# Two more products of the second feed-forward matmul split a second time, in five of eight blocks

## The chip, the core and the metric

The kernel runs on one core of a Trainium2 chip. Its engines are called PE (TensorE, matmuls), DVE (VectorE), ACT (ScalarE), POOL (GpSimd) and SP (SyncE, which here only issues DMAs). All five take their own instructions in order and wait for each other through semaphores. The metric is device time in microseconds (us). "Span" is the time from the first to the last instruction of the profiled execution.

## What is computed

One conditioned transformer block over x of shape (2, 2048, 512) in float32, with weights that the inputs give:

```python
emb = jnp.dot(jax.nn.silu(t), ada_w) + ada_b
shift_msa, scale_msa, gate_msa, shift_mlp, scale_mlp, gate_mlp = jnp.split(emb, 6, axis=-1)
norm = _ln(x) * (1.0 + scale_msa[:, None]) + shift_msa[:, None]
h = jax.nn.gelu(jnp.dot(norm, ssm_w1) + ssm_b1, approximate=False)
ssm_out = jnp.dot(h, ssm_w2) + ssm_b2
x = x + gate_msa[:, None] * ssm_out
norm2 = _ln(x) * (1.0 + scale_mlp[:, None]) + shift_mlp[:, None]
hf = jax.nn.gelu(jnp.dot(norm2, ff_w1) + ff_b1, approximate=True)
ff_out = jnp.dot(hf, ff_w2) + ff_b2
x = x + gate_mlp[:, None] * ff_out
```

ssm_w1 and ssm_w2 are 512 x 512, ff_w1 is 512 x 1024, ff_w2 is 1024 x 512.

## The kernel before

The 4096 rows are cut into 8 blocks of 512; blocks 0 to 3 belong to the first batch row, 4 to 7 to the second. The gates of a batch row are multiplied into ssm_w2 and ff_w2, so that the weights are reloaded and folded once in between. The order of the work is written out by hand (`manual_schedule`): what is emitted first stands first in its engine's queue.

All matmuls are float32, and none is done in the plain way. A product of two matrices, each cut into quarters, is made from seven products P1 to P7 of sums of quarters instead of eight. Sums of operands are made by POOL or DVE (`sums_of_first`, `sums_of_second`, 4 instructions each); the seven results are added up in PSUM banks y, x and v, which are read while they grow: `ORDER` gives the order P1, P2, P6, P5, P7, P3, P4 and `BANK` the bank of each. Some banks are "seeded": ACT writes the bias row into them first (`seed`).

Four stages make a block, and in the loop over i (blocks 1 to 7) those of different blocks are interleaved, in this order on PE:

- hC of block i, the first feed-forward layer (`Second.products`), by 26 products out of a deeper scheme. Their operands, 20 "forms", are made by `sums_of_registers` from the normalised block. DVE and ACT add the results up (lines 895 and 898), and ACT applies the gelu (876).
- oA of block i+1, the second matmul of the SSM part with its residual (`residual`).
- oC of block i, the second feed-forward matmul with its residual (`residual_in_leaves`, or `residual` in block 0).
- hA of block i+2, the first matmul of the SSM part (`First`).

So the residual stage oC of block 6 is followed by hC of block 7 at once, since there is no block 8.

In oC, `residual_in_leaves` makes P1, P5 and P6 as plain products (8 matmuls of 128 x 256 results each, line 724), each read by DVE (735). P2, P3 and P4 are split once more in the same manner. Each then has seven "leaves" of two matmuls with 128 x 128 results (757). They go in seven rounds of the order `LEAVES`: round 0 has the leaf P1 of all split products, round 1 the leaf P2, and so on. After P2's and P3's leaf DVE reads both (773), after P4's leaf it reads that (776). P7 is plain; its 8 matmuls are spread over rounds 0 to 3, and DVE reads it in round 4. The operand sums of the leaves are made by `leaves_of_weight` (once per batch row, into `fw2_t`) and `leaf_sums` (per block, into room in `forms`, or two `big` tiles in block 6).

"Hooks" are lists of instructions that are emitted behind a named product or round: `hook(hooks, ("P7",), ops)`. By them the other blocks' work is placed: statistics of the two normalisations (499, 500), their scales on POOL (508 to 526), the normalisation on ACT (539), transposes on DVE (550), the moves (559, 16 DMAs, SBUF to SBUF, that finish the transpose), the modulation on ACT (582), operand sums (347), forms (819), loads and stores on SP (203, 805).

x of a block is loaded once (203) and kept in a tile of the pool `big` (8 slots) until the block's result is stored; the normalised form nT gets a slot of its own. Other tiles of `big` are hA, hClo, hChi and, at the start, the ada weights.

## Time and profile before

| what | us |
|---|---|
| median of 3 runs | 594.32 |
| lowest and highest | 593.11, 594.48 |
| the profiled execution | 592.64 |
| its span | 590.8 |
| PE busy in it | 581.2 |
| DVE, ACT, POOL busy | 402.6, 236.0, 396.1 |

In block 2 the four stages last, and keep the engines busy, as follows (stretches of the span; POOL's spans are rough):

| stage | from, to | length | DVE | ACT | POOL |
|---|---|---|---|---|---|
| oA of block 3 | 223.50, 235.58 | 12.08 | 5.62 | 4.44 | 10.66 |
| oC of block 2 | 235.58, 258.77 | 23.19 | 15.32 | 6.70 | 9.58 |
| hA of block 4 | 258.77, 270.87 | 12.10 | 9.06 | 4.33 | 9.33 |
| hC of block 3 | 270.87, 293.35 | 22.48 | 15.34 | 15.29 | 22.01 |

PE is busy through the whole of each. In the rows of the profile a line's columns are the source line, the engine, the operation, the tile written and the tiles read, shapes, the count, busy time and mean duration; in a timeline the first two numbers are the start and the length, and the bracket is the idle time before it and what ended it. PE's matmuls overlap in the records, so that their price is the distance between starts.

### The profile page before, as it was taken

Reading aid. Unit: us, or ns where it says so; the run is one execution under the profiler, and the core shown is the slowest. Engines: PE = TensorE matmul, PEld = TensorE weight load, DVE = VectorE, ACT = ScalarE, POOL = GpSimd, SP = SyncE. Lnnn points to the kernel's source line nnn. Section 1 sums busy time; section 2 is a strip of 40 time slices with the busy share of each in tenths; the row PEclk is TensorE's granted clock in tenths of the full one; section 3 lists DMA queues with packets and bytes.
Section 4 is the critical chain, followed back from the end, with each engine's and each line's share of the span. In section 5 each row is a group of like instructions: output and inputs, shape, how many; then the busy total and the mean of one; then the engine's idle time right before and its main releaser. Section 6 shows DMA issues by size and latency. Waiting matters only on the chain.

```text
span 590.8 us, 8982 instructions
## 1 busy us (share of the span) xinstructions
PE 581.2 (98%) x3127; PEld 512.9 (87%) x3127; DVE 402.6 (68%) x723; ACT 236.0 (40%) x400; POOL 396.1 (67%) x480
## 2 busy tenths in 40 slices
PE   7999999999999999999999999999999999998997
PEld 4888888888889888998889988898888988897886
DVE  4978888897567475675755778874756446569663
ACT  2235457305532364234721456124553236222420
POOL 1875359999980968539984599948687294804260
PEclk9999999999999999999999999999999999999999
DMA  8990333300324104440152702231030400031002
GB/s 317 395 388 11 86 72 79 101 37 36 72 73 116 46 0 103 155 136 2 24 137 60 226 1 50 94 72 72 1 72 1 143 2 1 1 72 71 1 1 72
DMA packets 24376, 50.17 MB, mean 85 GB/s; under 512 B 4576, under 2 KB 5644, under 8 KB 23436
## 3 DMA queue, kind: packets, MB, share of 16 engines
q1 hardware_dynamic: 20608, 44.86, 24.5%
q10 hardware_dynamic: 3724, 4.75, 3.3%
q8 instruction: 25, 0.41, 0.3%
q14 instruction: 19, 0.16, 0.1%
HBM read 26.51 MB, written 8.40 MB: 59 GB/s over the span
## 4 chain that ended last, share of the span: by engine, by line
PE 95%; DVE 2%; DMA 2%; SPq 0%; issue 0%
PE py_oC L724 12%; PE px_hC L881 10%; PE py_hA L465 9%; PE py_oA L465 9%; PE py_hC L881 8%; PE pv_hC L881 8%; PE pl_oC_P_y L757 6%; PE pv_hA L465 5%; PE pv_oA L465 5%; PE pv_oC L724 4%; PE pl_oC_P_v L757 3%; PE px_hA L465 2%; PE py_oC L465 2%; PE py_hC L465 2%; PE px_oA L465 2%; DMA ada<-in_L_cond_ada_w_dram 2%
## 5 line engine op out<-in xcount | busy, mean ns | idle before, releaser
L582 ACT ACTIVATE nT<-nT,mod,mod 128x512 f32<-128x512 f32 x54 | 39.6, 803 | 103.0 <-DMA nT<-blocks 54.1
L539 ACT ACTIVATE nT<-x,nmr,rstd 128x512 f32<-128x512 f32 x56 | 42.5, 804 | 52.9 <-POOL nmr L526 38.0
L724 PE MATMUL py_oC<-fw,hClo 128*128 128x256 f32 x224 | 54.1, 379 | 0.0
L508 POOL TENSOR_SCALAR ve<-mv 128x4 f32<-128x4 f32 x16 | 3.7, 232 | 72.4 <-DVE mv L500 65.7
L499 DVE BATCH_NORM_STATS2 st<-x 128x6 f32<-128x512 f32 x64 | 43.4, 678 | 5.2 <-DMA x<-in_x_dram 4.9
L347 POOL TENSOR_TENSOR hSC<-hClo,hChi 128x512 f32<-128x512 f32 (+1 forms) x17 | 20.5, 1213 | 37.9 <-ACT hChi L876 24.4
L724 PEld LDWEIGHTS py_oC<-fw,hClo 128*128 128x128 f32 x224 | 40.4, 190 | 4.3
L881 PE MATMUL py_hC<-forms,fw 128*128 128x256 f32 x168 | 40.8, 379 | 0.0
L898 DVE TENSOR_TENSOR hClo<-hClo,py_hC 128x512 f32<-128x512 f32 x42 | 28.5, 681 | 17.3 <-ACT hClo L895 9.6
L819 POOL TENSOR_TENSOR forms<-forms 128x256 f32<-128x256 f32 x51 | 38.1, 748 | 3.0
L550 DVE STREAM_TRANSPOSE blocks<-nT 128x512 f32<-128x512 f32 x56 | 38.0, 695 | 1.6 <-ACT nT L539 1.2
L819 POOL TENSOR_TENSOR forms<-nT,forms 128x256 f32<-128x256 f32 x38 | 27.7, 749 | 15.9 <-DVE forms L819 15.4
L881 PEld LDWEIGHTS py_hC<-forms,fw 128*128 128x128 f32 x168 | 31.8, 190 | 4.4
L687 DVE TENSOR_TENSOR x<-py_oA,x 128x512 f32<-128x512 f32 x32 | 22.0, 688 | 19.4 <-PE py_oA L465 14.3
L898 DVE TENSOR_TENSOR hChi<-hChi,pv_hC 128x512 f32<-128x512 f32 x35 | 23.3, 683 | 14.3 <-PE pv_hC L881 14.3
L465 PE MATMUL py_hA<-nT,w 128*128 128x256 f32 x128 | 30.4, 380 | 0.0
L881 PE MATMUL px_hC<-forms,fw 128*128 128x256 f32 x112 | 27.8, 380 | 2.1 <-DVE forms L819 2.1
L876 ACT ACTIVATE hClo<-hClo,colsT 128x256 f32<-128x256 f32 x56 | 25.3, 500 | 4.9 <-DVE hClo L898 4.4
L895 ACT ACTIVATE hClo<-px_hC 128x512 f32<-128x512 f32 x21 | 12.5, 597 | 35.0 <-PE px_hC L881 30.1
L465 PE MATMUL py_oA<-w,hA 128*128 128x256 f32 x112 | 26.5, 379 | 0.0
L465 PEld LDWEIGHTS py_hA<-nT,w 128*128 128x128 f32 x128 | 23.7, 190 | 3.1 <-DVE hA L639 0.2
L876 ACT ACTIVATE hChi<-hChi,colsT 128x256 f32<-128x256 f32 x56 | 25.1, 496 | 1.9 <-DVE hChi L898 1.9
(291 smaller groups left out, 1584.0 us busy)
## 6 DMA issues: line engine op xcount, KB each, us to landing
nT<-blocks SPq DMA_DIRECT2D x168, 64.0 KB
x<-in_x_dram SPq DMA_DIRECT2D x7, 1024.0 KB
out_dram<-x SPq DMA_DIRECT2D x14, 512.0 KB
ada<-in_L_cond_ada_w_dram SPq DMA_DIRECT2D x6, 1024.0 KB
fw<-in_L_cond_ff_w_dram SPq DMA_DIRECT2D x2, 2048.0 KB
nT<-blocks ACTq DMA_DIRECT2D x56, 64.0 KB
w<-in_L_cond_ssm_w_dram SPq DMA_DIRECT2D x3, 1024.0 KB
fw<-in_L_cond_ff_w_dram SPq DMA_DIRECT2D x2, 1024.0 KB
```

The lines of the kernel that those rows point to most:

```text
L465: nc.tensor.matmul(ps[b][j * apart][:, j, :], lhs(p, j, k), rhs(p, j, k), start=(fresh and j * (not apart) == 0 and k == 0), stop=(p in (" ...
L499: nc.vector.bn_stats(st, xs[self.i][:, c, :])
L539: nc.scalar.activation(t, x_c, AF.Identity, bias=self.nmr[:, c : c + 1], scale=self.rstd[:, c : c + 1])
L550: nc.vector.transpose(self.bl[:, :, :, c, :].rearrange("p m k q -> p k m q"), self.nT[:, c, :].rearrange("p (k m q) -> p k m q", k=KD, m=C),)
L582: nc.scalar.activation(dst, src, AF.Identity, bias=shift, scale=scale)
L687: nc.vector.tensor_tensor(d, ps[BANK[p]][:, js], d, ALU.add)
L724: yield lambda j=j, k=k: nc.tensor.matmul(ps[BANK[p]][:, j, :], hops(p, j, k), wops[p][:, k, :], start=False, stop=(k == kdim - 1), skip_g ...
L757: nc.tensor.matmul(t[:, n, :], hops.leaves["P4" if which == "P4" else ("P2", "P3")[n]][f][:, k, :], leaf_wops["P4" if which == "P4" else ( ...
L819: eng.tensor_tensor(reg[d], reg[a], reg[b], ALU.add if f == "+" else ALU.subtract)
L876: nc.scalar.activation(h, h, AF.Gelu_apprx_tanh, bias=fb1T[:, m : m + 1])
L881: nc.tensor.matmul(ps[b][:, j, :], fa[ra][:, j * P : (j + 1) * P], fb[rb].rearrange("p a (c q) -> p c a q", q=Q), start=(fresh and j == 0) ...
L898: nc.vector.tensor_tensor(dest(d), dest(d), ps[b], op)
```

## The change

- In blocks 2, 3, 5, 6 and 7 (`five`) P5 and P7 are split into leaves too. Only P1 and P6 stay plain; P6 stands behind round 0. A round has ten matmuls; all leaves of a round are emitted first, then the readings. P5's leaves are read into two places with one instruction, as are P7's; P1+P6 goes into the lower rows with one wide instruction behind round 2. Blocks 1 and 4 keep three split products.
- P7's leaves share P4's banks. P5's chain has a part of the seeded bank v and parts of P4's banks; ACT writes a bias row (`leaf_row`, made by `apart_leaves`) into P4's bank v.
- Operand sums: P5's are made together with P3's, behind the scales of the second normalisation; P7's (`sums7`) are made by POOL in oA, in blocks 6 and 7 by DVE. The weight's new sums (`later`) are made by DVE in the following hA and hC.
- From block 2 on, the first normalisation writes into the tile of x itself. x is loaded again at the start of hC (`load_x(i + 1)`). The first load moves from P1 to P5 of oC. `big` has 7 slots; `brows` lies in `fw2_t`.
- Moved: the statistics of the first normalisation from oC to hA, its scales to hC, its normalisation and transposes to later places in hC; the modulation of the second one and its transposes to other places in oC; the reload of ff_w2 behind the last leaves; all 20 forms of block 7 into oC of block 6, 4 on DVE and 16 on POOL (12 and 8 before). In hA ACT takes the first reads of P6 and P5.

The diff, cut to its core:

```diff
-    big = ctx.enter_context(tc.tile_pool(name="big", bufs=8))
+    big = ctx.enter_context(tc.tile_pool(name="big", bufs=7))
...
+        for j, (p, w) in enumerate((("P4", s[:, 2]), ("P5", s[:, 0]), ("P7", lo[:, :, D // 2 :]))):
+            q, t = {n: v[:, :, 0, :] for n, v in views(w).items()}, thirds(fw2_t[:, 2 + j])
+            ops[p] = second_operands(q, t)
+            sums[p] = sums_of_second(q, t, engs[p])
...
+    def apart_leaves(row, eng):
+        a, b = slice(D // 2, D // 2 + P), slice(D // 2 + P, D)
+        eng.tensor_tensor(leaf_row[:, 2], row[:, b], row[:, a], ALU.subtract)
...
-                self.nT = big_tile(f"nT{self.name}")
+                in_place = self.which == 1 and self.i >= 2
+                self.nT = xs[self.i] if in_place else big_tile(f"nT{self.name}")
...
+        place = {("P2", b): (rooms["P23", b], 0) for b in "yxv"}
+        place |= {("P3", b): (rooms["P23", b], 1) for b in "yxv"}
+        place |= {("P4", b): (rooms["P4", b], 0) for b in "yxv"}
+        place |= {("P7", b): (rooms["P4", b], 1) for b in "yxv"}
+        place |= {("P5", "y"): (seeded, 0), ("P5", "v"): (rooms["P4", "v"], 2), ("P5", "x"): (rooms["P4", "x"], 2)}
...
+        if five:
+            places = {1: ("P6",), 2: ("P5",), 3: ("R2",), 4: ("P7",), 5: ("R4", "P3"), 6: ("P4",)}
         for r, f in enumerate(LEAVES):
             t, e = LEAF_AT[f]
-            for n in range(2):
-                leaf("P23", n, f)
-            d = xt[:, t, :].rearrange("p (q d) -> p q d", q=2)[:, :, e * P : (e + 1) * P]
-            nc.vector.tensor_tensor(d, leaf_ps["P23", LEAF_BANK[f]][:, :2, :], d, ALU.add)
-            leaf("P4", 0, f)
-            d = xt[:, 2 + t, e * P : (e + 1) * P]
-            nc.vector.tensor_tensor(d, leaf_ps["P4", LEAF_BANK[f]][:, 0, :], d, ALU.add)
-            if r == read_p7:
+            for p in ("P2", "P3"):
+                leaf(p, f)
+            if five:
+                p5, p4, p7 = [leaf(p, f) for p in ("P5", "P4", "P7")]
+            else:
+                p4 = leaf("P4", f)
+            add(X[:, 0, t, :, e, :], place["P2", LEAF_BANK[f]][0][:, :2, :])
+            if five:
+                add(X[:, :, t, 1, e, :], p5)
+            add(X[:, 1, t, 0, e, :], p4)
+            if five:
+                add(X[:, 1, t, :, e, :], p7)
+            if five and r == 0:
+                run(plain("P6"))
+                hooked("P2")
+            if five and r == 1:
+                read("P6", "12")
+            if five and r == 2:
+                nc.vector.tensor_tensor(
+                    xt[:, 2:4, :].rearrange("p t (q d) -> p t q d", q=2),
+                    ps["y"].unsqueeze(2).to_broadcast([P, 2, 2, F]),
+                    xt[:, 2:4, :].rearrange("p t (q d) -> p t q d", q=2),
+                    ALU.add,
+                )
+            if not five and r == 4:
                 read("P7", "22", "21")
...
     for i in range(1, NBLK):
+        five = i % PER_B != (1 if i < PER_B else 0)
...
+        elif not five:
+            hook(hooks, (7, 9), unread_stats)
+        else:
+            hook(hooks, (0, 1, 3, 5, 7), later)
+            later = []
         if nxt:
+            hook(hooks, (0,), [lambda: load_x(i + 1)])
             hook(hooks, (1, 2, 3, 4), hA[i + 1].summed(nc.gpsimd))
+        if nx2 and i > 1:
+            hook(hooks, (5,) if five else (9,), [n1[i + 2].scales])
...
+            at = (12, 14, 16, 18) if i == 1 else (15, 17, 19, 21) if five else (18, 19, 20, 21)
+            hook(hooks, at, [lambda c=c: n1[i + 2].normal(c) for c in range(C)])
+            hook(hooks, [n + 2 for n in at], [lambda c=c: n1[i + 2].turn(c) for c in range(C)])
...
-        sums24, sums3 = hC.leaf_sums(*hC.leaf_room(nxt, nx2), nc.gpsimd)
+        engs = (nc.gpsimd, nc.gpsimd, nc.gpsimd if nx2 else nc.vector)
+        sums24, sums35, sums7 = hC.leaf_sums(nxt, nx2, five, engs)
         hook(hooks, ("P5",), sums24)
-        hook(hooks, ("P7",), sums3)
+        if last or not five:
+            hook(hooks, ("P7",), sums35)
+        else:
+            hook(hooks, ("P7",) if nx2 else ("P5", "P7", "P7", "P3"), sums7)
...
-            hook(hooks, ("P1",), [lambda: load_x(i + 3)])
+            hook(hooks, ("P5",), [lambda: load_x(i + 3)])
+        if last:
+            hook(hooks, ("P1",), sums7)
...
+            if five:
+                hook(hooks, ("P1",), sums35)
             hook(hooks, ("P1",), [lambda c=c: n2[i + 1].normal(c) for c in range(C)])
-            turns = (("P6",) if leaf_fold else ("P2", "P2", "P6")) if nx2 else ("P1",)
+            turns = (("P6",) if leaf_fold else ("P2",) if five else ("P2", "P2", "P6")) if nx2 else ("P1",)
...
-            hook(hooks, ("P5", "P7", "P3", "P4"), n1[i + 3].stats())
-            hook(hooks, ("P4",), [n1[i + 3].scales])
...
-            hook(hooks, ("P7",), [lambda: load_half("fw2", fw2, fw2_sb, 0)])
...
-                        late["ops"] = form((nc.vector,) * 12 + (nc.gpsimd,) * 8)
+                        late["ops"] = form((nc.vector,) * 4 + (nc.gpsimd,) * 16)
                     late["ops"][n]()
-                late_forms = [lambda n=n: late_form(n) for n in range(len(HK_B))]
-                hook(hooks, ("P7",) * 4 + ("R4",) * 4, late_forms[:8])
-                late_forms = late_forms[8:]
+                hook(hooks, ("R2",), [lambda n=n: late_form(n) for n in range(len(HK_B))])
...
         if refold5:
+            load_half("fw2", fw2, fw2_sb, 0)
             load_half("fw2", fw2, fw2_sb, 1)
+            store(i, 0)
...
+        if i + 3 < NBLK:
+            st = n1[i + 3].stats()
+            unread_stats = st[2:] if refold5 else []
+            hook(hooks, ("P7", "P4") if refold5 else ("P5", "P7", "P3", "P4"), st[:2] if refold5 else st)
         if nx2:
-            hA[i + 2] = First(i + 2, n1[i + 2].ops, hooks)
+            hA[i + 2] = First(i + 2, n1[i + 2].ops, hooks, on_act=("P6", "P5"))
```

## The prediction

> **What bounds the kernel now.** I read the shares of the engines first, then TensorE's waits, then its order of work in one block, then DVE and GpSimd in the two places where the change puts work on them.

> ```profile
> span 590.8 us, 8982 instructions
> PE 581.2 (98%) x3127; PEld 512.9 (87%) x3127; DVE 402.6 (68%) x723; ACT 236.0 (40%) x400; POOL 396.1 (67%) x480
> ...
> PE 95%; DVE 2%; DMA 2%; SPq 0%; issue 0%
> ...
> PE px_hC L881 <- DVE forms L819: 2.1, 1, 2.1
> PE pada L274 <- DMA ada<-in_L_cond_ada_w_dram: 1.7, 2, 1.5
> PE idle L970 <- POOL ident masks.py:199: 1.3, 1, 1.3
> ```

> TensorE is 98% busy, the chain that ended last is 95% TensorE, and its waits come to 5.1 us: 3.0 in the first 12 us, then one of 2.1. The granted clock is 1.0. So what the change takes from TensorE's queue comes off the end, and what it makes TensorE wait for goes on. The single wait lies where block 7's first-layer products follow block 6's residual at once, with no other block's work between.

> ```profile
> 235.58 3.62 PE L724 MATMUL py_oC<-fw,hClo 128*128 128x256 f32 x16
> 239.04 3.62 PE L724 MATMUL pv_oC<-fw_s,hSC 128*128 128x256 f32 x16
> 242.49 3.62 PE L724 MATMUL py_oC<-fw_s,hSC 128*128 128x256 f32 x16
> 245.94 0.61 PE L757 MATMUL pl_oC_P_y<-fw,hChi 128*128 128x128 f32 x4
> ...
> 250.35 1.50 PE L757 MATMUL pl_oC_P_y<-fw_t,forms 128*128 128x128 f32 x12
> 251.69 1.03 PE L724 MATMUL py_oC<-fw,hClo 128*128 128x256 f32 x4
> ```

> This is the residual stage of block 2 (235.58 to 258.77, 23.19 us). Each matmul of the program leaves two records. A plain product, 8 matmuls of 256 columns, runs from 239.04 to 242.49: 3.45 us, 0.431 each. Six leaf matmuls of 128 columns run from 250.35 to 251.69: 1.34 us, 0.223 each. The starts show the price; the durations overlap.

> **The sum, TensorE.** A product costs 3.45 us plain and 14 x 0.223 = 3.12 as leaves, 0.33 less. The listing of the two programs' instructions agrees with the diff: 80 matmuls of 256 columns fewer, 140 of 128 more. That is 80 x 0.431 - 140 x 0.223 = 3.3 us. Only P1 and P6 stay plain, so the first leaf starts at T+3.45 (T is the stage's start) instead of T+10.36; a round of leaves is 10 matmuls, 2.23 us; P6's 3.45 stand behind round 0.

> **DVE in the rounds.** A round's reading was 0.42 + 0.29 us (rows L773, L776); now four reads, three of 256 elements, one of 128: starts 0.45, 0.34 and 0.31 apart and 0.42 for the last, 1.5 us. The plain reads of P5 and P7 (four of 0.69) go, one read of 1024 elements (about 1.3, as two of 0.69 took 1.28) comes. The stage then has some 7 x 1.5 + 2 x 0.69 + 1.3 + 2.7 (statistics) + 2.8 (transposes) = 18.7 us of DVE in 22.5, against 15.3 in 23.2. Bank y is written in rounds 0, 2, 4 and 6 and v in 3 and 5, so that one round lies between a round and the reads that it waits for (before round 2 also P6). For block 2: round 0's reads T+5.7 to 7.2; the transposes follow ACT's normalisation (GpSimd's scales ended T+6.4 in this trace, so T+10.1); round 1's reads T+11.4 to 12.9, P6's to 13.6; round 2's to 15.1, the wide read to 16.4; round 3's to 17.9, and round 5, which waits for them, would start at T+18.05. Round 4 waits for 15.1 and starts at 15.8. I take no stall, but the margins are 0.1 to 0.7 us. If round 3's reads are late, round 5 is late by as much.

> **GpSimd.** Its sums for P7 (4 of 0.73) take the place in the projection stage that P3's had; P3's and P5's become 4 of 1.27, and run behind the scales, T+6.6 to 11.7. TensorE wants the second of them in round 2 (T+11.4; done T+9.2) and the last in round 5. The forms for the next block then have their input earlier than now: in this trace they began at 263.86, behind scales that waited for DVE's statistics for 13.2 us. These scales move to the next block's products. From the moves: transposes end T+10.1, issue 6.3 to 6.6, landing 1.7 (as at 248.07 to 256.40), so forms from about T+21.5 against T+28.3. No cost.

> **DMA and queues.** x is loaded again (six DMAs of 1 MB on SP), first thing in the block's products, 34 us before its first reader; SP then stands idle there until the moves. The first load of x moves behind eight moves on SP, in front of the stores. It waits for those moves: issue about T+18.4, and 1 MB at the 188 to 293 GB/s that the windows around 324 to 328 show takes 4 to 5.5 us: T+24. Its first reader, DVE's statistics, now stands at T+29.4. The fw2 reload goes behind the last leaves that read it; its two halves land near T+25 and T+28, its reader stands at T+29.4. Taken at nothing; uncovered, each microsecond that DVE waits there holds up the hA sums queued behind it.

> **ACT and slots.** ACT takes two of DVE's first reads of the hA sums (20 halves in all, 0.42 to 0.47 each) and a copy of the leaf bias (under the 0.57 of a 512-wide one). In hA, P6's read on ACT ends 6.2 us into the stage, by the rows at 263.16 (gelu, 0.63) and 271.06 (two reads, 0.84); P7 would overwrite it at 6.9: a cover of 0.7 us. One slot fewer for the large tiles: the reload waits for the store of the block before last, over 10 us earlier. Both at nothing.

> **Block 6 into 7.** Here DVE's queue decides.

> ```profile
> 531.75 1.00 DVE L584 TENSOR_SCALAR nT<-nT,mod,mod 128x512 f32<-128x512 f32 x2
> 533.13 0.42 DVE L773 TENSOR_TENSOR x<-pl_oC_P_v,x 128x256 f32<-128x256 f32 x1 [0.38 <-PE pl_oC_P_v L757]
> ...
> 564.04 0.69 DVE L347 TENSOR_TENSOR hSC<-hClo,hChi 128x512 f32<-128x512 f32 x1
> 564.77 0.69 DVE L347 TENSOR_TENSOR hSC<-hSC,hClo 128x512 f32<-128x512 f32 x1
> 565.38 1.75 DVE L347 TENSOR_TENSOR hClo<-hClo 128x512 f32<-128x512 f32 x1
> 567.06 1.75 DVE L347 TENSOR_TENSOR hSC<-hChi,hSC 128x512 f32<-128x512 f32 x1
> 568.73 0.68 DVE L735 TENSOR_TENSOR x<-py_oC,x 128x512 f32<-128x512 f32 x1
> ```

> Of the 20 forms, DVE keeps 4 and GpSimd takes 16, all hooked behind round 3. DVE's order there: round 3's reads (to about T+18.4, since P7's sums on DVE delay the statistics by about 1.5), two modulations (1.0), four forms (1.7), only then round 4's reads, from T+21.1. Round 6 waits for the first of these: T+21.6 instead of 20.3, 1.3 us. GpSimd's forms start at T+21.2; the product that waited 2.1 us needs the eleventh form, 7 x 0.75 = 5.2 later, at T+26.4, when it is due at 23.8 + 2.6 = 26.4. So 1.3 in place of 2.1. Bounds: 0.3, if DVE is not delayed and the forms take 0.70 each; 2.9, if they take the 0.88 seen at 535.21 to 537.81 (2.59 for three) and DVE is 0.7 later still.

> **Last block.** The same rows show that a DVE sum of two SBUF operands takes 0.69 us alone and 1.75 while GpSimd sums. P1's read ended at 569.4, 6.2 us behind the stage's start at 563.21; P6, which waits for it, is now due at T+5.7: 0.5 us. Behind it stand P7's four sums on DVE, 0.42 each alone, about 1.0 by that ratio, then round 0's reads. Bounds 0 and 1.5.

> [...]

> **Small terms.** At the end one read of 0.42 stands where one of 0.29 did: +0.1. The weights' new sums (5 on DVE early in block 2's products, 0.42 to 0.8 each) fill gaps of 2.9, 0.3 and 0.7 us and make one read about 0.1 late; with the other blocks' moved statistics 0.2, bounds 0 and 1.

> Sum: -3.3 - 2.1 + 1.3 + 0.5 + 0.1 + 0.2 = -3.3 us. The profiled execution took 592.64 us (span 590.8 and 1.84 around it), 1.7 under the median of 594.32; the terms are taken from the median: **591.0**, a span of about 587.5.

> **Rivals.**
> 1. Nothing new waits: DVE's delays in blocks 6 and 7 stay at their low bounds. -3.3 - 2.1 + 0.3 + 0.1 = -5.0: 589.3. For it: the margins are estimates either way, and GpSimd alone made forms at 0.70. Against: DVE's reads of round 4 do stand behind forms.
> 2. The rounds become DVE's: in each of the five blocks rounds 4 to 6 start 0.5 to 0.7 us late, since round 3's reads end 0.1 us before they are wanted. 5 x 0.6 = 3.0 given back: 594.0. For it: 18.7 of 22.5 us; against: the first four matmuls of a round need only the first of four reads, a cover of 0.9 us.
> 3. Slower: the moved first load of x. If it lands later than T+29.4, DVE stands at the statistics, the hA sums behind them wait, TensorE stops. That needs 5 us more than my T+24; it decides in four blocks, and each microsecond beyond costs four. Two microseconds beyond, plus the DMA bytes that delay the moves: +8 - 3.3 = +4.7: 599. For it: the load and its moves share a queue that waits in order, and 1 MB more goes through it per block. Against: DMA share was 0.3 to 0.5 in these stages.

> **How the numbers follow.** My case 0.45 (590 to 592.4), rival 1 0.20, rival 2 0.20, rival 3 0.15. A measurement tells about 0.3%, 1.8 us, from no change: faster is below 592.5, cases mine and 1, 0.65; within, rival 2, 0.20; slower 0.15. The range 588.8 to 595.0 holds mine, rival 1 but for its end, and rival 2; what it leaves out is rival 3 and a little below, under 0.2. My case's own range is 590.0 to 592.4.

> **What would show it.** Right: the residual stage of blocks 2, 3 and 5 lasts 22.5 us instead of 23.2, blocks 1 and 4 keep 23.2; TensorE's waits list one before round 6 of block 6 of about a microsecond, on an L795 read, and one before P6 of the last block; no wait on DMA. Rival 2 shows as waits of leaf matmuls on L795 in every five-product block. Rival 3 shows as DVE waiting for an x load at the statistics. I am wrong at the root if the leaf pitch rises above 0.223, or if the five blocks' stages are no shorter than 23.2.

## The result and the profile after

The changed kernel took 595.72 us in the median (595.07 to 597.37, 13 runs) against 594.44 for the kernel before (592.85 to 596.16, 13 runs): a ratio of 1.0027, 95% interval 1.0015 to 1.0039. The forecast was 591.0. The profiled execution took 597.37 us, with a span of 595.2; it was the longest of the 13.

The page of the changed kernel first: the span, the engines' busy time, and the shares of the chain that ended last.

```profile
span 595.2 us, 9335 instructions
PE 581.6 (98%) x3247; PEld 517.2 (87%) x3247; DVE 434.5 (73%) x784; ACT 244.7 (41%) x425; POOL 424.2 (71%) x503
...
PE 78%; DVE 9%; POOL 5%; issue 3%; DMA 2%; ACT 1%; SPq 0%; DVEq 0%; POOLq 0%; ACTq 0%
```

TensorE is as busy as it was (98%), but the chain no longer runs through it at 95%: DVE and GpSimd have 14% of it. They made TensorE wait in new places, which the view of its waits lists (total, times, longest).

```profile
PE pl_oC_P_y L781 <- DVE x L795: 3.6, 3, 2.5
PE pada L275 <- DMA ada<-in_L_cond_ada_w_dram: 2.6, 2, 1.5
PE idle L1026 <- POOL ident masks.py:199: 1.3, 1, 1.3
PE px_hC L932 <- DVE hChi L949: 0.8, 1, 0.8
PE py_oC L735 <- DVE x L746: 0.6, 1, 0.6
```

The old wait of 2.1 us in block 7 is gone. Where the time went shows when the starts of the stages of both profiles are set side by side (us; each length is the next stage's start less its own).

| stretch | before | after | difference |
|---|---|---|---|
| start, to block 0's first-layer products | 70.75 | 72.60 | +1.85 |
| block 1's products | 22.46 | 23.84 | +1.38 |
| residuals of blocks 2, 3 and 5, each | 23.19 | 22.54 | -0.65, three times |
| block 4's products | 22.49 | 22.78 | +0.29 |
| block 4's residual | 23.29 | 24.40 | +1.11 |
| block 6's residual | 23.19 | 27.11 | +3.92 |
| block 7's products | 24.79 | 22.45 | -2.34 |
| block 7's residual, to the end of the span | 27.76 | 28.02 | +0.26 |

With -0.15 in the stages not listed this is the +4.4 us between the spans of 590.8 and 595.2. So the gain came as forecast, and new delays ate it: in block 1, in block 4, the largest in block 6 and a small one in block 7. The start is another matter, taken up at the end.

Two pieces of the table belong to this execution and not to every one: 1.85 us at the start and, shown below, 1.48 in block 6, both with a granted clock under 1.0. Eight of the 13 runs have a mean granted clock of 1.0, so they lost nothing to the clock; they took 595.07 to 595.88 us, where the profiled execution less the two pieces would be 594.0. What made them longer than that is not shown: no trace of such a run was kept. A late start at a full clock would be one way; e3's profile has one, with block 0's first-layer products at 71.80.

The residual of block 2 begins and ends here, before (its first row stands in the prediction, at 235.58) and after:

```profile
258.77 1.89 PE L465 MATMUL py_hA<-nT,w 128*128 128x256 f32 x8
```

```profile
238.78 3.62 PE L735 MATMUL py_oC<-fw,hClo 128*128 128x256 f32 x16
...
261.32 1.89 PE L474 MATMUL py_hA<-x,w 128*128 128x256 f32 x8
```

These are the late places in TensorE's order of work:

```profile
140.04 2.33 PE L932 MATMUL px_hC<-forms,fw_s 128*128 128x256 f32 x8 [0.79 <-DVE hChi L949]
...
393.34 1.58 PE L781 MATMUL pl_oC_P_y<-fw_t,forms 128*128 128x128 f32 x12 [0.98 <-DVE x L795]
...
528.55 0.61 PE L781 MATMUL pl_oC_P_x<-fw,hClo 128*128 128x128 f32 x4
531.63 2.05 PE L781 MATMUL pl_oC_P_y<-fw_t,leaves 128*128 128x128 f32 x8 [2.47 <-DVE x L795]
533.47 1.06 PE L781 MATMUL pv_oC<-fw_t,leaves 128*128 128x128 f32 x4
534.32 1.18 PE L781 MATMUL pl_oC_P_y<-fw_t,leaves 128*128 128x128 f32 x8
```

The last four lines hold more than the wait. Round 2 of block 6 was due at 529.00 (528.55 and 0.45 for four records) and began at 531.63, 2.63 late. Then its first 20 records took 3.71 us (531.63 to 535.34) where 20 at 0.1115 take 2.23: another 1.48 us, and the granted clock in the window from 531 to 535 is 0.57. In this execution a wait of 2.5 us cost 4.1.

What is late in each place is read on the other engines. In block 1 it is ACT, which waits for a store:

```profile
138.66 0.60 ACT L946 ACTIVATE hClo<-px_hC 128x512 f32<-128x512 f32 x1 [2.23 <-DMA out_dram<-x]
```

hClo of block 1 was given the room of x of block 0, and may be written only when the store of x has landed. In block 4 it is GpSimd:

```profile
346.90 1.28 POOL L348 TENSOR_TENSOR hSA<-hA,hSA 128x512 f32<-128x512 f32 x1
353.33 0.23 POOL L517 TENSOR_SCALAR ve<-mv 128x4 f32<-128x4 f32 x1 [5.16 <-DVE mv L509]
...
356.36 2.36 POOL L348 TENSOR_TENSOR fw_s<-fw 128x1024 f32<-128x1024 f32 x1
```

The scales, moved here by the change, wait 5.16 us for DVE's statistics, and the four sums of the folded weight (2.36 us each) stand behind them. Everything that follows on GpSimd is a microsecond late relative to its stage, down to the scales whose transposes precede round 0's reads. In block 6 DVE's order of work has the cause; GpSimd's stands below it, and then DVE's four scale instructions before the change:

```profile
515.85 1.48 DVE L348 TENSOR_TENSOR hClo<-hClo 128x256 f32<-128x256 f32 x1
...
521.98 0.67 DVE L746 TENSOR_TENSOR x<-py_oC,x 128x512 f32<-128x512 f32 x1
523.53 1.22 DVE L525 TENSOR_TENSOR e<-r,ve 128x4 f32<-128x4 f32 x1 [0.88 <-POOL r L519]
524.79 0.16 DVE L526 SCALAR_TENSOR_TENSOR e<-e,r 128x4 f32<-128x4 f32 x1
524.99 1.12 DVE L527 SCALAR_TENSOR_TENSOR rstd<-e,r 128x4 f32<-128x4 f32 x1
526.14 1.19 DVE L528 SCALAR_TENSOR_TENSOR nmr<-mv,rstd 128x4 f32<-128x4 f32 x1
528.35 2.82 DVE L560 STREAM_TRANSPOSE blocks<-nT 128x512 f32<-128x512 f32 x4 [1.02 <-ACT nT L549]
531.10 0.38 DVE L795 TENSOR_TENSOR x<-pl_oC_P_y,x 128x256 f32<-128x256 f32 x1
```

```profile
523.47 1.26 POOL L348 TENSOR_TENSOR leaves<-hSC,hSC 128x512 f32<-128x512 f32 x1
524.81 1.27 POOL L348 TENSOR_TENSOR leaves<-leaves,hSC 128x512 f32<-128x512 f32 x1
526.04 1.26 POOL L348 TENSOR_TENSOR hSC<-hSC 128x512 f32<-128x512 f32 x1
527.27 1.27 POOL L348 TENSOR_TENSOR leaves<-hSC,leaves 128x512 f32<-128x512 f32 x1
```

```profile
519.83 0.16 DVE L516 TENSOR_TENSOR e<-r,ve 128x4 f32<-128x4 f32 x1 [0.35 <-POOL r L510]
520.03 0.16 DVE L517 SCALAR_TENSOR_TENSOR e<-e,r 128x4 f32<-128x4 f32 x1
520.22 0.16 DVE L518 SCALAR_TENSOR_TENSOR rstd<-e,r 128x4 f32<-128x4 f32 x1
520.42 0.16 DVE L519 SCALAR_TENSOR_TENSOR nmr<-mv,rstd 128x4 f32<-128x4 f32 x1
```

Three of the four scale instructions, on four elements for each partition, take 1.1 to 1.2 us; before the change each took 0.16. GpSimd ran its sums for P3 and P5 (1.27 us each, 523.47 to 528.5) beside them: each of the three ends 0.02 to 0.03 us behind one of these sums, and the one that took 0.16 started 0.02 ahead of the next sum. The chain of four took 3.8 us (523.53 to 527.33) instead of 0.75, so that the transposes are 3 us late by it, and round 0's reads, for which round 2 waits, stand behind the transposes. P7's sums on DVE (the first line is the longest of them) had already made the statistics 1.1 us late: they end 4.4 us into the stage, before the change 3.3.

### The profile page after: what moved, and what is told of

Its sections match the earlier page's. It is cut to its first block, busy times and chain, and to the rows that moved or that the text cites. A ratio compares the mean times of both kernels' runs of the same rounds, so it can differ in the third digit from the quotient of the medians.

```text
span 595.2 us, 9335 instructions
## 1 busy us (share of the span) xinstructions
PE 581.6 (98%) x3247; PEld 517.2 (87%) x3247; DVE 434.5 (73%) x784; ACT 244.7 (41%) x425; POOL 424.2 (71%) x503
## 4 chain that ended last, share of the span: by engine, by line
PE 78%; DVE 9%; POOL 5%; issue 3%; DMA 2%; ACT 1%; SPq 0%; DVEq 0%; POOLq 0%; ACTq 0%
PE py_hA L474 9%; PE px_hC L932 8%; PE py_oA L474 8%; PE pv_hC L932 7%; PE py_hC L932 7%; PE pl_oC_P_y L781 6%; PE py_oC L735 6%; PE pv_hA L474 4%; PE pl_oC_P_v L781 4%; PE pv_oA L474 4%; PE py_hC L474 2%; PE px_hA L474 2%; PE px_oA L474 2%; PE pl_oC_P_x L781 2%; DMA ada<-in_L_cond_ada_w_dram 2%
## 5 line engine op out<-in xcount | busy, mean ns | idle before, releaser
L592 ACT ACTIVATE nT<-nT,mod,mod 128x512 f32<-128x512 f32 x30 | 22.0, 803 | 56.3 <-DMA nT<-blocks 42.4
L870 POOL TENSOR_TENSOR forms<-forms 128x256 f32<-128x256 f32 x55 | 41.4, 752 | 3.2
L870 POOL TENSOR_TENSOR forms<-nT,forms 128x256 f32<-128x256 f32 x41 | 30.1, 757 | 13.6 <-DVE forms L870 13.1
L549 ACT ACTIVATE nT<-x,nmr,rstd 128x512 f32<-128x512 f32 x32 | 23.4, 803 | 39.7 <-POOL nmr L535 30.6
L949 DVE TENSOR_TENSOR hClo<-hClo,py_hC 128x512 f32<-128x512 f32 x42 | 28.5, 684 | 15.3 <-ACT hClo L946 9.5
L795 DVE TENSOR_TENSOR x<-pl_oC_P_y,x 128x256 f32<-128x256 f32 (+1 forms) x76 | 28.0, 370 | 9.4 <-PE pl_oC_P_y L781 7.6
L735 PE MATMUL py_oC<-fw,hClo 128*128 128x256 f32 x144 | 33.6, 379 | 0.0
L592 ACT ACTIVATE x<-x,mod,mod 128x512 f32<-128x512 f32 x24 | 17.6, 802 | 38.8 <-DMA x<-blocks 38.8
L870 POOL TENSOR_TENSOR forms<-nT 128x256 f32<-128x256 f32 x12 | 9.1, 756 | 30.8 <-DMA x<-in_x_dram 18.8
L735 PEld LDWEIGHTS py_oC<-fw,hClo 128*128 128x128 f32 x144 | 26.8, 190 | 3.3
L949 DVE TENSOR_TENSOR hChi<-hChi,pv_hC 128x512 f32<-128x512 f32 x35 | 23.2, 680 | 7.0 <-PE pv_hC L932 6.9
L735 PE MATMUL py_oC<-fw_s,hSC 128*128 128x256 f32 x112 | 25.4, 380 | 0.6 <-DVE x L746 0.6
```

The costliest lines, as they stand in the source:

```text
L549: nc.scalar.activation(t, x_c, AF.Identity, bias=self.nmr[:, c : c + 1], scale=self.rstd[:, c : c + 1])
L592: nc.scalar.activation(dst, src, AF.Identity, bias=shift, scale=scale)
L735: yield lambda j=j, k=k: nc.tensor.matmul(ps[BANK[p]][:, j, :], hops(p, j, k), wops[p][:, k, :], start=False, stop=(k == kdim - 1), skip_g ...
L795: nc.vector.tensor_tensor(d, src, d, ALU.add)
L870: eng.tensor_tensor(reg[d], reg[a], reg[b], ALU.add if f == "+" else ALU.subtract)
L949: nc.vector.tensor_tensor(dest(d), dest(d), ps[b], op)
```

## Experiments

Each is the changed kernel with one edit, or several. The times stand against the kernel before, run on the same chip (594.43 in the median for the first four, 594.06 for the next four). The changed kernel was not run again beside them; its 595.72 is from the first set of runs, in which the kernel before had 594.44. The intervals reach 0.6 to 1.0 us to either side, so that gains of a microsecond or less are read from the stages of the profile.

**e1: the room of hClo_1.** A write of one column into hClo_1, while block 0's residual still runs, ties it to the room that hClo_0 leaves.

```diff
+    ahead_1 = Second(1)
+    hook(hooks, ("P3",), [lambda: nc.gpsimd.memset(ahead_1.lo[:, 0, :1], 0.0)])
     residual("oC_0", 0, hC, fw2_ops, KH // 2, hooks)
...
-        hC = Second(i)
+        hC = Second(i) if i > 1 else ahead_1
```

> Block 1's tile hClo_1 is placed in the room that hClo_0 leaves, by one small memset into it while block 0's residual still runs; the reloaded x_2 then takes the room of x_0, whose store ends late. Theory (rooms): in the changed kernel ACT waited 2.23 us for the store of x_0 before it could write hClo_1, and TensorE lost 1.4 us behind it (matmuls that started 2.81 us apart in block 0's pace started at 140.04 and 142.20 instead of 139.09 and 140.81). With the room free the two start on time: no wait of TensorE on hChi in block 1, median 1.4 us lower, 594.3. Rival (next in line): the reload of x_2 now waits for that store and holds up what stands behind it on SP, or DVE is what is late and px_hC still waits 0.5 us or more; the median stays at 595.3 to 595.8.

Measured: 594.13 us (ratio 1.0005, 0.9993 to 1.0017), 1.6 below the changed kernel. Block 1's products are 22.58 us long, and TensorE's waits no longer list px_hC. The reload of x_2, which now waits for the store in its turn, held up nothing. The theory holds.

**e2: half of the fold ahead of the scales in block 4.**

```diff
+        if fold:
+            hook(hooks, (5,), fold[3:5])
...
-            hook(hooks, (9,), fold[3:7])
+            hook(hooks, (9,), fold[5:7])
```

> In block 4's first-layer products two of GpSimd's four sums of the folded weight (2.4 us each) go ahead of the scales, into the 5.16 us in which GpSimd waited for DVE's statistics. Theory (GpSimd late by 1 us in block 4): everything behind the sums on GpSimd moves forward by 3 us or more, the scales of the second norm are ready earlier, the transposes start by T+11.5 instead of T+12.6 (T is the start of block 4's residual), the wait of 0.98 us at the leaf round 2 of block 4 goes; median 1.1 us lower, 594.6. Rival: the wait is set by something else on DVE (its four sums for P4's weights, 0.41 to 1.13 each), and stays at 0.7 us or more although GpSimd is early; median 595.4 to 595.9.

Measured: 594.94 us (1.0020, 1.0007 to 1.0032), 0.8 lower. In the profile GpSimd begins the sums at 348.92 in a stage that starts 0.5 us later than in the changed kernel, block 4's residual is back at 23.19 us, and the wait in its round 2 is gone. Block 5's products became 0.3 us longer, so that 0.8 is left of 1.1. The rival is out: DVE's four sums for P4's weights keep their place and take 3.0 us in all against 2.8, and the wait is gone all the same.

**e3 and e4: block 6, two ways.** The first, e3, puts GpSimd's sums for P3 and P5 ahead of the scales and leaves P7's on DVE; the second, e4, takes P7's sums off DVE and leaves those for P3 and P5 beside the scales. They part the two things that DVE met.

```diff
 # the first
-        if last or not five:
+        ahead = nxt and not nx2
+        if last or not five or ahead:
             hook(hooks, ("P7",), sums35)
-        else:
+        if five and not last:
             hook(hooks, ("P7",) if nx2 else ("P5", "P7", "P7", "P3"), sums7)
...
-            if five:
+            if five and not ahead:
                 hook(hooks, ("P1",), sums35)
 # the second
-        engs = (nc.gpsimd, nc.gpsimd, nc.gpsimd if nx2 else nc.vector)
+        engs = (nc.gpsimd, nc.gpsimd, nc.vector if last else nc.gpsimd)
...
-            hook(hooks, ("P7",) if nx2 else ("P5", "P7", "P7", "P3"), sums7)
+            hook(hooks, ("P7",), sums7)
```

> In block 6 alone the four sums for P3 and P5 on GpSimd (1.27 us each) go ahead of the second norm's scales instead of behind them, into the 5.1 us in which GpSimd waited for DVE's statistics. Theory (collision): in the changed kernel DVE's four small scale instructions took 1.22, 0.16, 1.12 and 1.19 us beside these sums where before the change each took 0.16; without the sums beside them they take 0.16 to 0.2 again, the transposes start about 3 us earlier, round 2's wait of 2.47 us falls to 0.5 or less, and the matmuls behind it don't run slow; median 2.5 to 3 us lower, 593.0. Rival (statistics): what is late is DVE's statistics, behind P7's sums (1.19, 0.89, 1.48 and 0.41 us); then the wait stays at 1.2 us or more and the median is 594.5 or above.

> In block 6 alone P7's four sums go from DVE to GpSimd, behind the sums for P2 and P4; the sums for P3 and P5 stay behind the scales. Theory (collision): DVE's statistics end 1.3 us earlier, but its four small scale instructions still run beside the sums for P3 and P5 and take about 1.1 us each; round 2's wait falls from 2.47 to about 1.2 us; median 594.4. Rival (statistics): the wait goes altogether, 0.3 us or less, and the median is 593.0.

Measured: 593.14 us (0.9984, 0.9974 to 0.9995) for the first, 2.6 below the changed kernel; 594.68 us (1.0019, 1.0006 to 1.0033) for the second, 1.0 below it. DVE's scale instructions in the first:

```profile
523.14 0.17 DVE L525 TENSOR_TENSOR e<-r,ve 128x4 f32<-128x4 f32 x1 [0.88 <-POOL r L519]
523.34 0.16 DVE L526 SCALAR_TENSOR_TENSOR e<-e,r 128x4 f32<-128x4 f32 x1
523.53 0.16 DVE L527 SCALAR_TENSOR_TENSOR rstd<-e,r 128x4 f32<-128x4 f32 x1
```

and in the second:

```profile
520.54 1.23 DVE L525 TENSOR_TENSOR e<-r,ve 128x4 f32<-128x4 f32 x1 [0.35 <-POOL r L519]
521.80 0.16 DVE L526 SCALAR_TENSOR_TENSOR e<-e,r 128x4 f32<-128x4 f32 x1
521.99 1.12 DVE L527 SCALAR_TENSOR_TENSOR rstd<-e,r 128x4 f32<-128x4 f32 x1
```

In the second the statistics end 3.3 us into the stage instead of 4.4, and three of the four instructions still take 1.1 to 1.2 beside GpSimd's sums of 1.26 to 1.27 (520.48 to 525.55); in the first, where GpSimd's last sum ended at 521.47, ahead of the scales, the three shown take 0.16 to 0.17. The sums beside them are what slowed them, in this run as in the changed kernel. The wait at round 2 is under 0.1 us in the first and 1.34 in the second. In both a wait before round 6 comes up, of 1.47 and 1.56 us; in the changed kernel, where round 2 was already late, only 0.19 of it was left to see. No slow matmuls follow these shorter waits: the granted clock is 1.00 in every window from 500 to 550 us in both.

**e5: P6 of the last block a round later.**

```diff
-            if five and r == 0:
+            if five and r == (1 if last else 0):
```

and likewise its read (round 2 instead of 1) and the wide read (3 instead of 2).

> In the last block the plain product P6 stands behind round 1 of the leaves instead of round 0, and its read and the wide read each one round later. Theory (P1's read late): P6 waits for DVE's read of P1, which stands behind sums that share the time with GpSimd's; a round later it finds that read done, TensorE's wait of 0.57 us on py_oC goes, and the 0.73 us by which P6 started late with it; the median is 0.6 lower, 595.1, with the clock noise a difference that the profile shows better than the time. Rival (DVE is late as a whole): the wait goes to round 2 on DVE's reads of round 0, 0.4 us or more there, and the median stays at 595.4 to 595.9.

Measured: 596.18 us (1.0037, 1.0021 to 1.0053; 5 runs from 595.39 to 597.34): no gain that can be told. The wait on py_oC went, and 0.35 us of wait came at round 2, on round 0's reads, which stand behind P7's four sums on DVE (0.89, 1.37, 1.48 and 1.49 us). The last stretch is 0.2 us shorter. The rival holds: DVE as a whole is late there.

**e6: e1, e2, e3 and e5 together. e7: the same with block 6's scales on GpSimd.** In place of e3's edit, e7 has P7's sums of block 6 on GpSimd as well, and the sums for P3 and P5 behind the scales, as in blocks 2, 3 and 5 (e4's edit and this one).

```diff
-            hook(hooks, ("P1",), [lambda: n2[i + 1].scales(on_dve=not nx2)])
+            hook(hooks, ("P1",), [lambda: n2[i + 1].scales()])
```

> The room for hClo_1 (e1), the split fold (e2), the sums for P3 and P5 of block 6 ahead of the scales (e3) and P6 later in the last block (e5) together. Theory (the waits are separate and add up): 595.72 - 1.6 (e1) - 0.8 (e2) - 2.6 (e3) - 0.6 = 590.1; TensorE's remaining wait behind the start is the one before round 6 of block 6, 1.5 us. Rival (each wait hides the next): the gains overlap, and the median is 591.5 or above.

> As e6, but in block 6 the scales are worked out on GpSimd as in the other blocks, with P7's sums on GpSimd ahead of them and those for P3 and P5 behind them, so that DVE has neither the four sums nor the four small scale instructions. Theory (what is late at round 6 is DVE, by the 1.3 us that P7's sums cost it): statistics end at T+3.3 (T is the start of block 6's residual), scales at T+6.2, transposes at T+10, no wait at round 2, and the wait before round 6 falls from 1.5 to 0.3 us; median 588.9. Rival (the moves and the modulations set it): the wait before round 6 stays at 1 us or more, and the median is that of e6, 590.1, or above.

Measured: 591.13 us (0.9955, 0.9941 to 0.9970) and 589.71 us (0.9925, 0.9911 to 0.9939). e6 is a microsecond above its sum, of which 0.6 is the gain that P6 did not bring, and falls between theory and rival. e7 beats both kernels, the one before by 4.35 us in the median, and its five runs lie between 589.60 and 589.75. TensorE's waits in e7:

```profile
PE pada L275 <- DMA ada<-in_L_cond_ada_w_dram: 2.3, 2, 1.5
PE idle L1026 <- POOL ident masks.py:199: 1.3, 1, 1.3
PE pl_oC_P_y L781 <- DVE x L795: 1.3, 2, 0.9
```

Behind the start only 0.94 us before round 6 of block 6 and 0.35 in the last block are left. The 0.94 falls between theory (0.3) and rival (1 or more): with P7's sums and the scales off DVE the wait is 0.5 us shorter, and from the transposes to round 4's reads DVE works without a gap of note. The transposes begin 7.3 us into the stage, 0.9 later than before the change, since the scales take 3.06 us on GpSimd alone (517.04 to 520.10), where GpSimd and DVE took 2.13 before the change (518.45 to 520.58); how much of the 0.94 is this and how much DVE's own work behind them was not parted.

**e8: three blocks with fewer leaves.** As e6, with P5 and P7 plain in blocks 2, 3 and 5. The switch also moves these blocks' scales, normalisation, transposes and operand sums to the places that the code gives them in blocks with three split products. The first three of the eight sums of the reloaded fw2 for P5 and P7 are taken here before the gate is folded in, so that the output isn't the reference's; there are as many of them.

```diff
-        five = i % PER_B != (1 if i < PER_B else 0)
+        five = i % PER_B != (1 if i < PER_B else 0) and i not in (2, 3, 5)
```

> As e6, but blocks 2, 3 and 5 run P5 and P7 plain as blocks 1 and 4 do, so that only blocks 6 and 7 have them as leaves. Theory (price of a product): 3 blocks x (16 x 0.431 - 28 x 0.223) = 3 x 0.65 = 2.0 us slower than e6: 592.1. Rival (DVE bounds the rounds): if the reads behind all leaves cost as much as the leaves save, it is within 0.7 us of e6.

Measured: 594.40 us (1.0017, 1.0003 to 1.0031), 3.3 above e6. The three residuals are 23.19 us each, against 22.54: the 2.0 of the theory, so the leaves do save their price and DVE doesn't take it back. The other 1.3 us is not in these three stages: the wait before round 6 of block 6 grew to 2.12 us (why was not followed up), and the granted clock behind it is 0.83 in the window from 535 to 545 us.

**e9 and e10: the kernel before, profiled twice more.** No edit.

> The kernel before the change, looked at again. Its times fall into two groups, 592.7 to 593.7 us at a mean granted clock of 0.999 to 1.0 and 594.1 to 595.1 at 0.996 to 0.997; the profile shown of it is one of the first. Theory (a long wait costs clock): its one wait of 2.1 us in block 7 is followed in the slower group by some 3 us at about half the granted clock, 1.7 us in all, as the wait of 2.47 us was in the changed kernel (0.57 in the 4 us after it). A look in the slower group shows that clock there and 1.0 elsewhere behind the start. Rival (the start): the clock is lost in the first 20 us. A look in the faster group tells nothing apart.

> The same kernel once more, for a second chance at a look in the slower group: theory and rival as for the first look.

Measured: 592.72 and 594.32 us, one in each group. The windows from 543 to 547 us, just behind the 2.1 us wait, e9 and then e10 (the columns are window, length, busy time of PE, PEld, DVE, ACT and POOL with counts, the granted clock, the DMA share and GB/s):

```profile
543.00:547.00 4.00, 3.90 (x18) 3.49 (x19) 3.54 (x7) 0.60 (x1) 0.00 (x0) 1.00 0.10 39
```

```profile
543.00:547.00 4.00, 3.96 (x11) 3.30 (x12) 2.40 (x5) 0.60 (x1) 0.00 (x0) 0.57 0.09 34
```

18 matmul records in one and 11 in the other, at 1.00 and 0.57. Up to 500 us both have 1.00 and the same work. The spans differ by 1.6 us, and block 7's products last 24.79 and 26.47 us. The theory holds.

## Why the prediction was wrong

- **The products (part of -3.3).** Right: 22.54 against 23.19 us in each of blocks 2, 3 and 5, and the leaves stayed at 0.223 for each matmul. Blocks 1 and 4 kept plain products. Rival 2 (the rounds become DVE's) is out: no round of these three blocks waited.
- **The old wait (-2.1).** Right in kind, too small in size. Block 7's products lost 2.34 us in the profile; and in part of the runs of the kernel before that wait took a further 1.6 us by the clock, so its median, 594.4, holds more to be gained than the profile that I worked from, which stands at 592.64. Taking the terms from the median left that out.
- **"Here DVE's queue decides" (block 6).** This step failed most. I made the statistics 1.5 us late (1.1 measured), and then left the scales and transposes where they were, as if they followed at their old pace. But the change hooks the sums for P3 and P5 on GpSimd directly behind its part of the scales, and DVE's part runs at that very moment. I had shown that DVE's sums of two SBUF operands stretch beside GpSimd's, in the last block (1.75 us against 0.69), and applied it to long sums alone; here three of four instructions of 0.16 us took 1.12 to 1.22 beside GpSimd's sums of 1.26 to 1.27, and each of the three ended just behind one of these sums. P7's four sums on DVE took 4.0 us in block 6 and 5.2 in the last block. In the profiled execution the step cost 2.63 us of lateness and 1.48 of lower clock.
- **"1.3 in place of 2.1" (round 6).** Near in size, though hidden: 0.19 in the changed kernel, 1.47 and 1.56 once the earlier wait was smaller. That DVE's queue sets it was right. The size is in part luck: the working allows 0.3 if DVE is not delayed by P7's sums, and e7, without them on DVE, still waits 0.94.
- **"One slot fewer for the large tiles ... at nothing."** Failed, 1.4 us. I followed the one tile that is new, the reload of x, to its room; with one room fewer later tiles change rooms as well, and the one that got x_0's was hClo_1, whose first writer stood 2.2 us waiting for x_0's store.
- **"These scales move to the next block's products ... No cost."** Failed in block 4, 1.1 us. I looked at who would read the scales sooner or later, and not at what stands behind them in GpSimd's queue while they wait (5.16 us): e2, which puts half of that ahead of them, takes the wait of 0.98 us away.
- **The last block (+0.5).** Right in kind: 0.57 us of wait, P6 0.73 late. I had misread the stage's start, which is 563.04 and not 563.21, so that the same working gives 0.7. P7's sums on DVE, put at about 1.0 each, took 0.88 to 1.48.
- **Rival 3 (the first load of x).** Out: DVE's statistics wait for a load of x only at the very start, 4.96 us, as before the change (4.91).
- **Small terms (+0.2).** Near in size by luck: block 2's products, which have the weights' new sums, were no longer than before (22.45 against 22.49 us), and block 4's gave +0.29, whose cause was not looked for. Rival 1 (nothing new waits) is out with the waits above.

e7, without most of the waits that I had put at nothing, took 589.6 us in its profiled run against 592.64 for the kernel before, 3.0 less, where I had worked out 3.3. That supports the sum of the moved and removed work, but is no test of each term, since e7 also takes off DVE work from which the 1.3 was worked out. The forecast failed on three covers for which I named no row of the trace: e1, e2 and e3, which restore one each, measured 1.6, 0.8 and 2.6 us less, against the 4.7 by which the forecast was short.

## What to carry to other kernels

When work is moved beside other work, price every instruction that then runs on the two engines, the shortest first: here a chain of four small dependent steps took 3.8 us instead of 0.75, three of them 1.12 to 1.22 each beside the neighbour's sums of 1.26 to 1.27. A step at nothing needs its cover named for every user: when a room is taken away, list who gets which room anew; when an instruction that waits is moved, list what is queued behind it. And a gain may be real and still invisible: undo the new waits one by one before giving the idea up.

## What the runs showed of the hardware

In six of the twelve profiles a wait of TensorE of 2.1 to 2.5 us has a lower granted clock behind it, and so cost more than its length. Granted clock right behind the longest wait of block 6 or 7: 0.57 after 2.47 us (the changed kernel, and e2), 0.55 after 2.46 (e1), 0.57 after 2.46 (e5), 0.83 in a window of 10 us around 2.12 (e8), and both 1.00 and 0.57 after 2.1 us in e9 and e10; 1.00 after 1.47 (e3). Where the clock fell it cost 1.48 us in the changed kernel (20 records in 3.71 us instead of 2.23) and 1.68 in e10 against e9 (block 7's products, 26.47 and 24.79). The kernel before has its 49 times from the two sets of experiments in two groups, 592.7 to 593.7 at a mean granted clock of 0.999 to 1.0 (20 of them), and 594.1 to 595.1 at 0.996 to 0.997 (29); e7, whose longest wait behind the start is 0.94 us, has its five within 0.15 us.

Nine falls of the granted clock show in the windows ahead of the end of TensorE's work: two each in the changed kernel and e2, one each in e1, e5, e6, e8 and e10. Each took about 1.7 us of full clock (0.57 in 4 us, 0.79 in 8, 0.83 in 10, in e1 0.55 in 3 and 0.91 in the next 4). In the changed kernel's trace the record of the granted clock begins, full, at 5.50 us, and it is 0.5 for 3.413 us each from 12.33 and from 531.15: 6.83 and 525.65 us after its beginning, 2.0 and 154.0 times that length. In the kernel before it is full from 6.86, where the record begins, to 590.54: 171.0 times that length.

Open stays the start. The first products of block 0 began at 14.6 us in all three profiles of the kernel before, at 14.7 to 14.9 in five of the changed kernel's variants, and at 15.7 to 17.1 in the other three and in the changed kernel itself, three of these four with a granted clock of 0.79 between 9 and 17 us. In the changed kernel the 1.98 us ahead of its fall at 12.33 are waits for the ada weights, where the kernel before has 1.53 of them in one step. Whether the change has a part in that, by the rows that it loads into another tile (TensorE waited 0.5 to 1.6 us for them in three of the four, in e2, e3 and e6), wasn't tried.
